# A graph network kernel: the work ahead of the first one-hots put in one tied order

## The chip, the cores and the metric

The kernel runs on one core of a Trainium2 chip. The core has a matrix engine (TensorE, "PE" in the profile, its weight loads listed apart as "PEld"), a vector engine (VectorE, "DVE"), a scalar engine (ScalarE, "ACT"), GpSimd ("POOL", used here for index patterns and for indirect DMAs) and SyncE ("SP", used here only to issue DMAs). Each engine takes its instructions in the order in which the program was laid out. Time is device microseconds (us) of one execution. Before the change the median of 7 runs is 885.18 us, the lowest 883.09, the highest 887.0.

## The reference

Two graph layers stand one behind the other, on 6250 nodes with 64 features and 206250 edges, which are sorted by destination. The first layer is two graph convolutions, the second a message network; both need sums over the edges of a node.

```python
h = jnp.maximum(_layernorm(x, axis=-1), 0.0)
x = x + _L0_gnn_ref(h, edge_index, ...)      # two convolutions
h = jnp.maximum(_layernorm(x, axis=-1), 0.0)
x = x + _L1_gnn_ref(h, edge_index, ...)      # messages, their sum, an update

def _gin_conv(x, src, dst, Wa, ba, Wb, bb):
    agg = jax.ops.segment_sum(x[src], dst, num_segments=N)
    h = x + agg
    h = jax.nn.relu(h @ Wa + ba)
    return h @ Wb + bb

message = node_features[source]
y = _mlp3(message, WM1, bM1, WM2, bM2, WM3, bM3)
z = jax.ops.segment_sum(y, destination, num_segments=node_features.shape[0])
```

Every sum over edges is a product with one matrix A, whose element (source, destination) is the number of edges between the two. A has 6250 by 6250 elements.

## The kernel before

The nodes are cut into 49 tiles of 128 (`NT`). For each tile t of destinations the kernel builds its 49 blocks of A in bytes (`build`, L433), adds the first convolution's sum from them (`FirstSum`, L576) and stores the blocks to DRAM. Two later sweeps load A again for the other two sums (L760); they take the time from about 366 us on and are not touched.

**How a tile of A is built.** The edges of 64 pairs of nodes (`G`) are turned into one-hots on VectorE by `hot` (L404): "there" (L411), "high" (L415) and "low" (L418), one instruction each for a whole tile, and in three pieces of 16, 16 and 32 for tile 0 (`FIRST_HOTS`). TensorE multiplies low by high: 64 small matmuls for a tile in four groups of 16 (L443, "counts"). ScalarE copies each group out of PSUM (L445). After each group `between` issues one quarter of the previous tile's sum (L586, 12 or 13 matmuls with the values `hp`), and whatever stands in the table `beside` under that group's number, 4 t + i.

**Where the one-hots come from.** The edges of two tiles are found in these steps, for batches of 1, 2, 2, ... pairs of tiles (`BATCHES`): `search` (L301) compares every 550th destination with the tile's bounds on ScalarE and gets a row number on VectorE (L313, L314); `fetch_blocks` (L317) gathers that row by an indirect DMA on POOL; `search_block` (L326) compares again on ScalarE; `fetch_edges` (L337) works out the offset on VectorE and gathers 128 destinations and sources by indirect DMAs (`d_win`, `s_win`); `slots` (L353) turns them into numbers by 9 to 11 VectorE instructions; `cast` (L389) copies two of the three numbers to bf16 on ScalarE; `turn` (L394) transposes them on TensorE, and ScalarE copies the result to `lkw` (L402), which `hot` reads. Batch 0 feeds tiles 0 and 1, batch 1 tiles 2 to 5.

**Where `hp` comes from.** The 49 tiles of x are taken in seven chunks of 7 (`values`, L507). `norm` (L232) is the layernorm: mean, a scale, the difference, a square on ScalarE, its sum, a root on ScalarE, a reciprocal, and the last product, so six VectorE instructions with two trips to ScalarE. `split` (L250) then writes h as three bf16 parts into `hp`: three ScalarE copies and, between them, products of TensorE with the identity (L256, fp32) and with minus the identity (L258) that leave the remainder. A product holds one of the two "cnt" buffers in PSUM, which the counts use too. Quarter 0 of a sum needs chunks 0 and 1, quarter 3 needs chunks 5 and 6.

**What sets the order.** The program is written as a list of calls; a planner at compile time places each instruction on its engine when, by its own estimates, its inputs are ready, earlier calls first. `behind(op, other)` ties an instruction behind another on the same engine without any wait at run time. `follow` ties one behind the newest count, copy or one-hot that is recorded in `counted`. At the start of the program (L546 to L572) come searches, the layernorm chunks 0 to 4 and the slots of batch 0, with few ties; chunks 5 and 6 come after tile 0 has been built, and the slots of batch 1 are in `beside` under the first group of tile 0.

Of the kernel before, what the change touches and what calls it, by code (L numbers as in the profile page):

```python
# [146 lines left out]
def load_x(nc, xs, x, engines):  # L147
# [5 lines left out]
    engines[0].dma_start(xs[:N - full * P, full, :], x[full * P:])  # L153
# [3 lines left out]
def fast(ctx: ExitStack, tc: tile.TileContext, x, src, dst, w, bad, out):  # L157
# [16 lines left out]


# [6 lines left out]
    load_x(nc, xs, x, [nc.sync, nc.scalar])  # L182
# [12 lines left out]
    nc.vector.tensor_scalar(ident_a, w.ident, 1.0 / UNIT, None, op0=OP.mult)  # L195
# [12 lines left out]
    nc.vector.tensor_copy(smp_f, smp_i)  # L208
# [23 lines left out]
    def norm(to, t, n):  # L232
# [10 lines left out]
        nc.vector.tensor_reduce(var, sq, axis=AX.X, op=OP.add)  # L243
        nc.scalar.activation(var, var, AF.Sqrt, bias=w.eps, scale=1.0 / D)
        nc.vector.reciprocal(var, var)
        nc.vector.scalar_tensor_tensor(to, xm, 0.0, var[:, :, None].to_broadcast([P, n, D]), op0=OP.max, op1=OP.mult)  # L246
        return begun, centered, squared

    def split(parts, h):
# [4 lines left out]
        for i in range(2):  # L254
            ps = banks[:, i].rearrange("p (t d) -> p t d", d=D)
            nc.tensor.matmul(ps, w.ident, h, start=True, stop=False)  # L256
# [26 lines left out]
    counted, swept = {}, []  # L283

    def behind(op, other):

        tc.add_manual_dep(op.ins, other.ins.name,
                          mybir.DependencyInfo(mybir.DependencyClass.NoSync, mybir.DependencyReason.DATA),
                          reason="order on an engine")
        return op  # L290
# [46 lines left out]
    def fetch_edges(b):  # L337
# [4 lines left out]
        nc.vector.scalar_tensor_tensor(off_f[:, qs], sign2[:, qs], -0.5, base[:, qs], op0=OP.mult, op1=OP.add)  # L342
# [10 lines left out]
    def slots(b):  # L353
# [12 lines left out]
        def first(op):  # L366
            follow(op, "DVE")

# [17 lines left out]
        nc.vector.tensor_tensor(byte, byte, shift, op=OP.logical_shift_left)  # L386
# [7 lines left out]
    def turn(b, i):  # L394
# [4 lines left out]
        for k in range(3):  # L399
            follow(nc.tensor.transpose(ps[:, k * P:(k + 1) * P], parts2[b % 2][:, i, k, :], identb), "PE")  # L400
# [3 lines left out]
    def hot(lkw, g0, n):  # L404

        def of(i):
# [4 lines left out]
        nc.vector.tensor_tensor(there, word2[:, None, :, :].to_broadcast(shape),  # L411
                                of(0)[:, :, None, :].to_broadcast(shape), op=OP.is_equal)
# [7 lines left out]
            of(2)[:, :, :, None].to_broadcast([P, n // 2, 2, W]), op=OP.mult)  # L420
        return low.bitcast(F8), high
# [10 lines left out]
    def build(t, between):  # L432
# [3 lines left out]
        for g0, m in FIRST_HOTS if t == 0 else ((0, G),):  # L436
            low, high = hot(lkw, (t % 2) * G + g0, m)
# [68 lines left out]

    def values(t):  # L507
        h = work.tile([P, XT, D], FP, name="h")
        begun, centered, squared = norm(h, t, XT)
        if t <= XT:  # L510
            behind(begun, sampled)
            behind(begun, bounds)
# [530 lines left out]
```

## Time and profile before

| | |
|---|---|
| median of 7 runs | 885.18 us (883.09 to 887.0) |
| the profiled execution | 884.99 us, of which the span of the trace is 882.3 us |
| busy, share of the span | TensorE 853.2 us, 97%; its weight loads 731.9 us, 83%; VectorE 629.9 us, 71%; ScalarE 570.4 us, 65%; POOL 122.5 us, 14% |
| lines that cost TensorE most | L760 (sweeps), L586 (first sums, 237.1 us), L443 (counts, 113.6 us), L256 (products of h, 17.5 us) |
| first group of counts starts | 33.37 us |
| tile 0's last copy of counts | 39.69 us |

The span begins with the first instruction and ends with the last; 2.7 us of the execution lie outside it. "Low of tile t" below is the last of the three one-hot instructions of a tile; its end is when the tile's counts can start. Averages over the whole span say little about the first 60 us, so the lines that matter are those of stretches of a few microseconds.

### The profile page before, as it was taken

How to read it: one execution, taken by the hardware profiler on the slowest of the kernel's cores; microseconds unless marked ns; L12 is line 12 of the kernel's file. 1: busy time of each engine (PE TensorE's matmuls, PEld its weight loads, DVE VectorE, ACT ScalarE, POOL GpSimd, SP SyncE). 2: the span in 40 equal slices, each digit the busy share in tenths (PEclk: the TensorE clock that was granted, in tenths of full speed). 3: DMA queues.
4: the chain of work that ended last, by engine and by line, in shares of the span. 5: the costliest groups of instructions: out<-in, count | busy, mean ns of one | idle time of the engine just before them, and what ended most of it. 6: DMA issues, size and time to landing. Idle time of an engine off the chain costs nothing.

```text
span 882.3 us, 19764 instructions
## 1 busy us (share of the span) xinstructions
PE 853.2 (97%) x8251; PEld 731.9 (83%) x8251; DVE 629.9 (71%) x933; ACT 570.4 (65%) x775; POOL 122.5 (14%) x86
## 2 busy tenths in 40 slices
PE   3799999999999999999999999999999999999997
PEld 1489999999999999888888878888889877777785
DVE  6999999999999998635554545554556686767672
ACT  5776777776776666655555555546546578878773
POOL 4537732324421200000000000000000000000000
PEclk9899999999999999999999999999999999999998
DMA  6336555455544543734444444334434567877772
GB/s 147 111 113 183 149 162 150 138 149 172 161 138 126 144 126 112 232 97 136 120 123 132 122 123 122 124 111 133 132 89 130 176 217 230 247 231 229 246 209 60
DMA packets 148326, 133.57 MB, mean 151 GB/s; under 512 B 29988, under 2 KB 110500, under 8 KB 148228
## 3 DMA queue, kind: packets, MB, share of 16 engines
q1 hardware_dynamic: 141784, 121.19, 46.3%
q0 software_dynamic: 3600, 10.32, 4.0%
q8 instruction: 66, 1.08, 0.5%
q10 hardware_dynamic: 2844, 0.72, 0.4%
q14 instruction: 32, 0.26, 0.1%
HBM read 91.25 MB, written 40.94 MB: 150 GB/s over the span
## 4 chain that ended last, share of the span: by engine, by line
PE 82%; DVE 6%; DMA 5%; ACT 4%; issue 1%; SPq 0%; POOL 0%; ACTq 0%; DVEq 0%; POOLq 0%
PE acc L760 42%; PE acc L586 20%; PE cnt L443 8%; PE ps_t L465 5%; DMA a<-A 4%; PE ps_y L474 3%; ACT ar L753 3%; DVE low L418 1%; PE ps_g L504 1%; DVE high L415 1%; DMA blk<-in_dst_dram,row 1%; DVE there L411 1%; PE cnt L256 1%; DVE ar L753 1%; DMA xs<-in_x_dram 1%
## 5 line engine op out<-in xcount | busy, mean ns | idle before, releaser
L753 DVE CAST ar<-a 128x2048 fp32r<-128x2048 uint8 (+1 forms) x200 | 220.1, 1110 | 183.5 <-PE acc L760 158.5
L753 ACT CAST ar<-a 128x2048 fp32r<-128x2048 uint8 (+2 forms) x126 | 232.4, 1846 | 123.8 <-PE acc L760 107.5
L760 PE MATMUL acc<-ar,h2r 128*128 128x512 f32 (+2 forms) x1274 | 297.6, 388 | 0.0
L760 PEld LDWEIGHTS acc<-ar,h2r 128*128 128x128 f32 x1274 | 229.3, 188 | 49.8 <-issue 5.8
L586 PE MATMUL acc<-hp,a 128*128 128x193 bf16 x2401 | 237.1, 248 | 0.4 <-ACT a L445 0.2
L445 ACT ACTIVATE a<-cnt 128x784 int16<-128x784 f32 x196 | 161.0, 822 | 70.0 <-PE cnt L443 69.8
L586 PEld LDWEIGHTS <-a 128*128 128x128 fp8e4 x2401 | 196.8, 98 | 2.6 <-issue 0.8
L760 PE MATMUL acc<-ar,yr 128*128 128x512 f32 (+2 forms) x637 | 157.6, 399 | 0.0
L760 PEld LDWEIGHTS acc<-ar,yr 128*128 128x128 f32 x637 | 115.7, 189 | 32.5 <-issue 10.1
L443 PEld LDWEIGHTS <-low 128*128 128x128 fp8e4 x3136 | 107.0, 96 | 9.4 <-issue 8.2
L443 PE MATMUL cnt<-high,low 128*128 128x49 bf16 x3136 | 113.6, 186 | 1.0 <-DVE low L418 0.5
L418 DVE TENSOR_TENSOR low<-there,lkw 128x2048 int32<-128x2048 bf16 (+2 forms) x51 | 112.1, 2197 | 0.0
L415 DVE TENSOR_TENSOR high<-high,lkw 128x3136 bf16<-128x3136 bf16 (+2 forms) x51 | 87.8, 1721 | 16.0 <-PE cnt L443 15.5
L322 POOL DMA_INDIRECT blk<-in_dst_dram,row x25 | 58.8, 2353 | 99.8 <-DVE base L314 87.3
L411 DVE TENSOR_TENSOR there<-word,lkw 128x2048 bf16<-128x2048 bf16 (+2 forms) x51 | 58.9, 1173 | 0.0
L347 POOL DMA_INDIRECT s_win<-in_src_dram,off x25 | 35.3, 1413 | 7.6 <-issue 7.6
L347 POOL DMA_INDIRECT d_win<-in_dst_dram,off x25 | 26.1, 1043 | 65.1 <-DVE pair L370 48.5
L256 PE MATMUL cnt<-h,ident 128*128 128x448 f32 x28 | 17.5, 725 | 11.5 <-DVE h L246 10.1
L467 ACT ACTIVATE t<-ps_t,d 128x512 f32<-128x512 f32 (+2 forms) x26 | 17.3, 664 | 11.2 <-PE ps_t L465 11.1
L467 ACT ACTIVATE t<-ps_t,c 128x512 f32<-128x512 f32 (+1 forms) x26 | 17.2, 663 | 9.1 <-PE ps_t L465 9.1
L333 ACT ACTIVATE junk<-blk,below_node 128x550 bf16<-128x550 int32 x25 | 18.7, 748 | 3.4 <-DMA blk<-in_dst_dram,row 3.4
L256 PEld LDWEIGHTS cnt<-h,ident 128*128 128x128 f32 x28 | 5.4, 232 | 17.9 <-issue 5.7
(125 smaller groups left out, 611.9 us busy)
## 6 DMA issues: line engine op xcount, KB each, us to landing
a<-A SPq DMA_DIRECT2D x276, 256.0 KB, 2.8
A<-a SPq DMA_DIRECT2D x49, 768.0 KB, 4.2
a<-A SPq DMA_DIRECT2D x24, 192.0 KB, 2.6
a<-A SPq DMA_DIRECT2D x22, 64.0 KB, 2.4
out_dram<-o SPq DMA_DIRECT2D x11, 128.0 KB, 3.0
A<-a SPq DMA_DIRECT2D x49, 16.0 KB, 3.9
xs<-in_x_dram ACTq DMA_DIRECT2D x3, 224.0 KB, 6.0
xs<-in_x_dram SPq DMA_DIRECT2D x3, 224.0 KB, 6.3
```

The lines of the kernel that those rows point to most:

```text
L322: nc.gpsimd.indirect_dma_start(out=blks[q], out_offset=None, in_=dst.rearrange("(r b) -> r b", b=BLK), in_offset=bass.IndirectOffsetOnAxis ...
L347: nc.gpsimd.indirect_dma_start(out=win[:, i, :], out_offset=None, in_=of.rearrange("(a o) -> a o", o=1), in_offset=bass.IndirectOffsetOnAx ...
L411: nc.vector.tensor_tensor(there, word2[:, None, :, :].to_broadcast(shape), of(0)[:, :, None, :].to_broadcast(shape), op=OP.is_equal)
L415: nc.vector.tensor_tensor(high, high2[:, None, :, :].to_broadcast(shape), of(1)[:, :, None, :].to_broadcast(shape), op=OP.is_equal)
L418: counted["DVE"] = nc.vector.tensor_tensor(low.rearrange("p (g i) w -> p g i w", i=2), there.rearrange("p g w i -> p g i w"), of(2)[:, :, ...
L443: counted["PE"] = nc.tensor.matmul(ps[:, b, j * H:(j + 1) * H], low[:, g, :], high[:, g // 2, :, g % 2], start=True, stop=True)
L445: counted["ACT"] = nc.scalar.activation(a[:, :, k:k + 2 * PG].rearrange("p h (b j) -> p h b j", b=2), ps[:, :, :PG * H].rearrange("p b (j ...
L465: placed(nc.tensor.matmul(ps[:, :n * P], wt, rhs, start=(i == 0), stop=(i == len(terms) - 1)))
L467: nc.scalar.activation(to, ps[:, :n * P], AF.Relu, bias=bias)
L586: nc.tensor.matmul(acc[:, t % 2, :], self.a[:, k, :], hp[:, k], start=(k == 0), stop=False)
L753: widen(ar.rearrange(f"p k t b -> {order}"), a.rearrange(f"p t (k b) -> {order}", b=P))
L760: op = nc.tensor.matmul(acc[:, :n * P], part, ar[:, k - k0].rearrange("p t b -> p (t b)"), start=(k == 0 and i == 0), stop=(k == H - 1 and ...
```

## The change

The change touches only the first two tiles' worth of work and leaves every computation as it was. It does these things:

- x is loaded on the two queues in the other order: chunks 0, 2, 4, 6 are issued by ScalarE, chunks 1, 3, 5 and the tail by SyncE.
- The first use of the sample of destinations (L208) is tied behind four small constants on VectorE.
- The products of h on TensorE (L256) are tied behind the newest transpose of `turn` and the newest count that has been issued by then.
- Chunks 0, 1 and 2 stay at the start, with chunk 0's mean behind the sample, its square behind the first search, and chunk 1's mean behind the first row number. Of chunk 3 only the mean and the difference stand ahead of the offsets of batch 1 and the slots of batch 0; its products come after batch 0's transposes.
- Chunk 4 is issued under the first group of tile 0: its mean behind the last slot instruction of batch 0, its variance behind the first low. The second piece of tile 0's one-hots is tied behind chunk 4's h.
- Chunk 5 is issued under the last group of tile 0, with its mean behind tile 0's last low. Chunk 6 is issued under the first group of tile 1, with its mean behind tile 1's low.
- The slots of batch 1, which stood under the first group of tile 0, are tied behind chunk 6's h; the casts and transposes of batch 1 move from tile 0's groups to groups 1 to 3 of tile 1.
- The searches and block searches of batches 2 and 3 move with them, into `beside` of tile 0.

The diff, cut to its core:

```diff
-    engines[0].dma_start(xs[:N - full * P, full, :], x[full * P:])
+    engines[-1].dma_start(xs[:N - full * P, full, :], x[full * P:])
...
-    load_x(nc, xs, x, [nc.sync, nc.scalar])
+    load_x(nc, xs, x, [nc.scalar, nc.sync])
...
-    nc.vector.tensor_scalar(ident_a, w.ident, 1.0 / UNIT, None, op0=OP.mult)
+    constants = nc.vector.tensor_scalar(ident_a, w.ident, 1.0 / UNIT, None, op0=OP.mult)
...
-    nc.vector.tensor_copy(smp_f, smp_i)
+    behind(behind(nc.vector.tensor_copy(smp_f, smp_i), constants), bounds)
...
-            nc.tensor.matmul(ps, w.ident, h, start=True, stop=False)
+            op = nc.tensor.matmul(ps, w.ident, h, start=True, stop=False)
+            for other in ("turn", "PE"):
+                if other in counted:
+                    behind(op, counted[other])
...
-    def fetch_edges(b):
+    def fetch_edges(b, before=None):
...
+        if before:
+            behind(op, before)
...
-    def slots(b):
+    def slots(b, before=None):
...
         def first(op):
             follow(op, "DVE")
+            if before:
+                behind(op, before)
...
+        counted["turn"] = op
...
-    def hot(lkw, g0, n):
+    def hot(lkw, g0, n, before=None):
...
+        if before:
+            behind(op, before)
...
-            low, high = hot(lkw, (t % 2) * G + g0, m)
+            low, high = hot(lkw, (t % 2) * G + g0, m, {0: normed[3][1], 16: normed.get(4, [None])[-1]}.get(g0) if t == 0 else None)
...
-    def values(t):
-        h = work.tile([P, XT, D], FP, name="h")
-        begun, centered, squared = norm(h, t, XT)
-        if t <= XT:
-            behind(begun, sampled)
-            behind(begun, bounds)
-            behind(squared, searched[0])
-        if t == XT:
-            behind(centered, searched[1])
-        split(hp[:, t:t + XT], h)
+    normed, hs = {}, {}
+
+    def values(c, *others, whole=True):
+
+        h = hs[c] = work.tile([P, XT, D], FP, name="h")
+        normed[c] = norm(h, c * XT, XT)
+        for op, other in zip(normed[c], others):
+            if other:
+                behind(op, other)
+        if whole:
+            parts_of(c)
+
+    def parts_of(c):
+        split(hp[:, c * XT:(c + 1) * XT], hs.pop(c))
...
-        at(0, slots, b + 1)
-        at(4, cast, b + 1, 0)
-        at(5, cast, b + 1, 2)
+        if b > 0:
+            at(0, slots, b + 1)
+        at(4 if b else 10, cast, b + 1, 0)
+        at(5 if b else 10, cast, b + 1, 2)
         for i in range(BATCHES[b + 1] if b + 1 < len(BATCHES) else 0):
-            at(7 + 2 * i, turn, b + 1, i)
+            at(7 + 2 * i if b else 12 + 2 * i, turn, b + 1, i)
...
-    values(0)
+    values(0, sampled, None, searched[0])
+    values(1, searched[1])
     search_block(0, 0)
     fetch_edges(0)
-    values(XT)
-    slots(0)
+    values(2)
+    for i in range(2):
+        op = search_block(1, i)
+    values(3, normed[2][-1], whole=False)
+    fetch_edges(1, normed[3][1])
+    slots(0, normed[3][1])
     cast(0, 0)
     cast(0, 2)
-    for i in range(2):
-        op = search_block(1, i)
-    fetch_edges(1)
     turn(0, 0)
-    values(2 * XT)
     search(2, op)
     fetch_blocks(2)
-    values(3 * XT)
-    search(3)
-    fetch_blocks(3)
-    values(4 * XT)
-    for i in range(2):
-        search_block(2, i)
-    fetch_edges(2)
+    parts_of(3)
+
+    def fourth():
+        normed[4] = None
+        values(4, counted["slots"], None, None, firsts[0])
+
+    def fifth():
+        values(5, counted["DVE"])
+
+    def sixth():
+        values(6, counted["DVE"])
+        slots(1, normed[6][-1])
+
+    beside[0] = [(fourth, ()), (search, (3,)), (fetch_blocks, (3,))] + beside.get(0, [])
+    beside[3] = [(search_block, (2, 0)), (search_block, (2, 1)), (fetch_edges, (2,)), (fifth, ())] + beside.get(3, [])
+    beside[4] = [(sixth, ())] + beside.get(4, [])
...
             if t == 0:
-                values(5 * XT)
                 for i in range(2):
                     search_block(3, i)
                 fetch_edges(3)
-                values(6 * XT)
                 search(4)
                 fetch_blocks(4)
```

More of the change, by code (lines that the diff above doesn't have):

```diff
@@ L173, in bank, with behind @@
         return pmix.tile([P, CH * 4 // mybir.dt.size(dtype)], dtype, tag="mix", name=name)
+    def behind(op, other):
+        tc.add_manual_dep(op.ins, other.ins.name,
+                          mybir.DependencyInfo(mybir.DependencyClass.NoSync, mybir.DependencyReason.DATA),
+                          reason="order on an engine")
+        return op
     root = const.tile([P, 1], FP, name="root")
@@ L242, in norm @@
         var = work.tile([P, n], FP, name="var", tag=f"var{n}")
-        nc.vector.tensor_reduce(var, sq, axis=AX.X, op=OP.add)
+        summed = nc.vector.tensor_reduce(var, sq, axis=AX.X, op=OP.add)
         nc.scalar.activation(var, var, AF.Sqrt, bias=w.eps, scale=1.0 / D)
         nc.vector.reciprocal(var, var)
-        nc.vector.scalar_tensor_tensor(to, xm, 0.0, var[:, :, None].to_broadcast([P, n, D]), op0=OP.max, op1=OP.mult)
-        return begun, centered, squared
+        ended = nc.vector.scalar_tensor_tensor(to, xm, 0.0, var[:, :, None].to_broadcast([P, n, D]), op0=OP.max, op1=OP.mult)
+        return begun, centered, squared, summed, ended
     def split(parts, h):
@@ L281, in tiles_of @@
         return range(starts[b], starts[b] + BATCHES[b]), slice(starts[b], starts[b] + BATCHES[b])
[L283 to L290, printed above, removed]
+    counted, firsts, swept = {}, [], []
     def follow(op, engine):
@@ L341, in fetch_edges @@
         each, qs = tiles_of(b)
-        nc.vector.scalar_tensor_tensor(off_f[:, qs], sign2[:, qs], -0.5, base[:, qs], op0=OP.mult, op1=OP.add)
+        op = nc.vector.scalar_tensor_tensor(off_f[:, qs], sign2[:, qs], -0.5, base[:, qs], op0=OP.mult, op1=OP.add)
+        if before:
+            behind(op, before)
         nc.vector.tensor_scalar(off[:, qs], off_f[:, qs], float(E - P), None, op0=OP.min)
@@ L385, in slots @@
         nc.vector.tensor_scalar(byte, byte, float(BYTE[1] - BYTE[0]), float(BYTE[0]), op0=OP.mult, op1=OP.add)
-        nc.vector.tensor_tensor(byte, byte, shift, op=OP.logical_shift_left)
+        counted["slots"] = nc.vector.tensor_tensor(byte, byte, shift, op=OP.logical_shift_left)
         numbers[b] = {0: word, 2: byte}
@@ L399, in turn @@
         for k in range(3):
-            follow(nc.tensor.transpose(ps[:, k * P:(k + 1) * P], parts2[b % 2][:, i, k, :], identb), "PE")
+            op = nc.tensor.transpose(ps[:, k * P:(k + 1) * P], parts2[b % 2][:, i, k, :], identb)
+            follow(op, "PE")
+        counted["turn"] = op
         lkw = lkws[starts[b] + i] = wins.tile([P, 3, P], BF, name="lkw", bufs=5)
         nc.scalar.copy(lkw.rearrange("p a b -> p (a b)"), ps[:, :3 * P])
-    def hot(lkw, g0, n):
+    def hot(lkw, g0, n, before=None):
         def of(i):
@@ L410, in hot @@
         there = hots.tile([P, G // 2, W, 2], BF, name="there")[:, :n // 2]
-        nc.vector.tensor_tensor(there, word2[:, None, :, :].to_broadcast(shape),
-                                of(0)[:, :, None, :].to_broadcast(shape), op=OP.is_equal)
+        op = nc.vector.tensor_tensor(there, word2[:, None, :, :].to_broadcast(shape),
+                                     of(0)[:, :, None, :].to_broadcast(shape), op=OP.is_equal)
+        if before:
+            behind(op, before)
         shape = [P, n // 2, H, 2]
@@ L420, in hot @@
             of(2)[:, :, :, None].to_broadcast([P, n // 2, 2, W]), op=OP.mult)
+        firsts.append(counted["DVE"])
         return low.bitcast(F8), high
```

## The prediction

> **What bounds the kernel now.** First the chain that ended last, in order of time. From 365 us on it is TensorE in the sweeps, which the change leaves alone; around 85 to 110 us it is TensorE's counts and first sums; between 57 and 85 us it is VectorE without a break:
>
> ```profile
> 59.61 0.34 DVE byte L386
> 59.95 1.13 DVE there L411
> 61.08 0.53 DVE r L594 x2
> 61.62 1.70 DVE high L415
> 63.32 2.20 DVE low L418
> ...
> 82.61 0.20 DVE byte L385
> 82.81 2.21 DVE low L418
> 85.02 0.05 issue
> 85.07 0.59 PE cnt L443 x16
> 85.66 1.11 PE acc L586 x13
> ```
>
> The reader sees that the low of tile 7, at 85 us, is what TensorE waits for last; after it TensorE never waits for a one-hot for long. So the end is set by when VectorE gets there. Second, VectorE's busy time in stretches (start:end, length, busy, instructions, clock, DMA share, GB/s):
>
> ```profile
> 5.40:12.00 6.60, 5.91 (x24) 1.00 0.87 152
> 12.00:26.00 14.00, 11.08 (x37) 1.00 0.45 122
> 26.00:33.00 7.00, 6.02 (x23) 1.00 0.51 155
> 33.00:40.00 7.00, 6.29 (x11) 0.76 0.18 56
> 40.00:45.00 5.00, 4.88 (x6) 0.66 0.58 161
> 45.00:51.65 6.65, 6.02 (x10) 1.00 0.10 30
> 51.65:60.00 8.35, 8.11 (x19) 1.00 0.60 175
> 60.00:84.93 24.93, 24.93 (x33) 1.00 0.55 161
> ```
>
> From the end of tile 2's low (49.37 + 2.28 = 51.65) to that of tile 7 VectorE idles 0.24 us in 33.3. Before it, from the landing of the sample at 5.4, it works 40.2 us and idles 6.05. Third, the timeline names those idle times and the waits of TensorE:
>
> ```profile
> 20.04 0.23 DVE L370 TENSOR_SCALAR pair<-d_win 128x128 int32<-128x128 int32 x1 [1.87 <-DMA d_win<-in_dst_dram,off]
> 32.06 1.02 PE L256 MATMUL cnt<-h,ident 128*128 128x448 f32 x2 [2.02 <-DVE h L246]
> 38.51 0.20 DVE L245 RECIPROCAL var<-var 128x7 f32<-128x7 f32 x1 [0.71 <-ACT var L244]
> 39.38 0.41 ACT L392 CAST parts<-byte 128x256 bf16<-128x256 int32 x1
> 40.40 0.48 ACT L402 COPY lkw<-ps_win 128x384 bf16<-128x384 bf16 x1
> 41.96 2.28 DVE L418 TENSOR_TENSOR low<-there,lkw 128x2048 int32<-128x2048 bf16 x1
> ```
>
> VectorE's 6.05 us are 0.53 for x, 0.69 for the first block, 1.87 for the destinations, 0.72, 0.71 and 0.63 for layernorm roots, and small ones. The counts of tile 0 are ready when the first low ends at 27.37, but start at 33.37, behind a product of h that waits 2.02 us. TensorE idles 2.89 + 1.31 + 0.41 + 0.26 = 4.9 us between 26 and 53.5.
>
> **The sum is made at one place:** low of tile 2 ends at 51.65 now. What follows to 84.93 is the same VectorE work in both kernels, so a later or earlier low of tile 2 moves the end by as much, as long as TensorE keeps up.
>
> **The parts in front.** Four constants leave the path between the sample and its product: 5.63 to 6.12, a gain of 0.5. The first search wins 0.2 more, since its row (L313, 9.85) waits now behind a mean. Chunk 0 of x is issued on ScalarE's queue at 0.74 instead of SyncE's at 1.81, landing 6.0 us after issue, so near 6.7 instead of 7.17. ScalarE issues one load more (0.44 to 0.84 each, ending about 3.4); it is idle until 8.38, so this costs nothing. SyncE's later weight loads come about 1.1 us sooner, and would cost only if they slowed the first gather (landing 3.9). The two gathers then cost what they did (10.28 to 14.15; 15.74 to 20.02), and the first slot instruction starts near 19.1 instead of 20.04. Slots of batch 0 run 1.9 us without the h, sum and difference that stand between them now (0.61 + 0.60 + 0.61), so they end near 21.2 instead of 23.64; cast, transposes and copy take 1.6 to 2.2 (23.64 to 25.87). The first low ends near 25, its counts start near 25.2 instead of 33.37, and tile 0 is counted some 6 us earlier. That is what the change does; it frees TensorE, not VectorE.
>
> **The part that costs.** The slots of batch 1 run now between 27.3 and 33.5, their copy is there at 40.88, and tile 2's one-hots wait for nothing. Afterwards they are behind chunk 6's h, and that chunk's mean is behind tile 1's low. So from tile 1's low to tile 2's this stands in a row:
> - chunk 6: mean to scale 0.66, scale to difference 0.20 (9.11, 9.77, 9.97), difference 0.61, square 0.57, sum 0.61, root 0.28, reciprocal 0.20, h 0.62, and five hand-overs of about 0.04: 3.95;
> - slots for two tiles: 77.80 to 79.29 and 0.20 + 0.21 + 0.20 + 0.41: 2.5;
> - cast, transposes, copy: 39.38 to 40.88, and 0.32 from copy to "there" (25.55 to 25.87), 0.05 in front: 1.87;
> - one-hots 1.14 + 1.70 + 2.28: 5.1.
>
> The sum is 13.4 us, against 51.65 - 44.24 = 7.41 now. VectorE is idle in it for square and root (1.0) and the 1.87, with little else that may run: chunk 5's last steps, offsets and rows. To break even tile 1's low has to end at 38.2 instead of 44.24.
>
> **The balance.** Idle time of VectorE up to tile 2's low, taken (and bounds):
> 1. for x: 0.5 (0.3 to 0.6), row 0.53.
> 2. up to the first slot: 2.9 (2.0 to 3.8), rows 0.69 and 1.87. The wait is 0.9 us shorter, but chunk 1's mean may not start before the first row number, so less stands ready.
> 3. for the first copy of `lkw`: 0.3 (0 to 0.8); chunk 4's mean and difference and chunk 3's end (about 2.6) cover the 2.2.
> 4. chunk 4's and 5's roots: 0.5 (0.2 to 1.5). They cost 2.45 with small ones now; the one-hots that are not tied fill them.
> 5. chunk 6: 1.3 (0.5 to 2.3): the 1.0, and one copy of counts (0.83) that may stand ahead of its square on ScalarE, less what fills it.
> 6. the turn of batch 1: 2.9 (1.6 to 4.5): the 1.87, and what TensorE has in front of the transposes. Chunk 6's product becomes ready with the same h (from 47.74 to 51.1 now: 3.4 us), the slots and cast take 2.9 of that; a quarter (1.02) may stand there as well.
>
> Together 8.4 (4.6 to 13.5) instead of 6.05. Work: 40.2 - 0.5 for the constants, + 1.0 because steps that depend on each other start after the full duration (0.61) and not after 0.53 as interleaved ones do (10.50 to 11.03); some 13 such steps: 40.7 (39.7 to 41.0). Tile 2's low ends at 5.4 + 40.7 + 8.4 = 54.5, or 2.9 us later. Against the profiled execution (884.99; span 882.3 and 2.7 around it) that is 887.9. That execution lies 0.2 under the median of the runs, so the forecast is 885.18 + 2.9 = 888.1. The likeliest case alone spans 887 to 890.5.
>
> **TensorE's cover.** The products move with the chunks and cost nothing, because TensorE will be ahead: tile 1's quarters (4.3 us), which stand after tile 2's first counts now, come before them. If that cover went (half clock, or counts and two products sharing the two "cnt" buffers), the cost would be what exceeds 4.3. A pair of product passes takes 1.02 at 32.06 and 1.86 at 34.16, while the clock row shows 0.76 and 0.66. Were chunks 3 to 6 all at the slow rate, TensorE would do 4 x 2 x 0.84 = 6.7 us more than at the fast one; part of it is paid now.
>
> [...]
>
> **Rivals.**
> - Faster: the gain on the first counts goes through. It decides where tile 2's low ends before 49.9 (1.8 us earlier), which needs an idle total of at most 3.8, or 4.8 with the work at its lower bound; the lower bounds sum to 4.6. So: the turn at 1.6 and chunk 6's waits filled by chunk 5's last steps, and a first wait under 2. For it: 2.45 us of root waits vanish. Against it: the 1.87 us after the slots have no cover. TensorE's 4.9 us of idle time are its ceiling, 880.3; I would expect 882.
> - No change: an idle total near 5.5, as the waits named in front go and those of chunk 6 and batch 1 come: 5.4 + 40.7 + 5.5 = 51.6, so 885.2. For it: tile 1's low at 38 to 38.5 is possible, since its work is 7 us nearer the front.
> - Much slower: the transposes of batch 1 stand behind tile 1's third group of counts, which needs a "cnt" buffer while chunks 5 and 6 hold them 3 to 4 us each, and behind two products and two quarters. Item 6 goes to 4.5 and 5 to 2.3, item 2 to 3.6: idle total 11.7, low at 57.8, 891.3.
>
> **How the numbers follow.** Chances: forecast 0.46, much slower 0.20, no change 0.20, faster 0.14. A difference of 0.2% (1.8 us) is about what a measurement of this kernel tells from none. So slower 0.66, same 0.20, faster 0.14. The range 883.5 to 892 leaves out about 0.1 at either end: most of the faster case, and the upper part of the much slower one.
>
> **What would show it.** Right: first counts near 25 us, tile 0's last copy near 33; tile 1's low near 39 to 41; then the two root waits of chunk 6 on VectorE, and a gap of 2 to 4 us ahead of tile 2's "there", released by ScalarE's `lkw`; tile 2's low near 54.5 and VectorE on the chain up to about 88. Wrong: tile 2's low before 50, or VectorE no longer on the chain after it, so that TensorE alone sets the end; or the first slot later than 20, because the gathers land later.

## The result, and the profile after

The changed kernel takes 891.12 us (median of 17 runs, 888.5 to 893.94), the kernel before beside it 885.0 (42 runs, 882.58 to 888.38): a ratio of 1.007, 95% interval 1.0061 to 1.008. In a second group of runs, with the experiments, it took 890.58 (6 runs) beside 886.32 (24 runs): 1.0048, interval 1.003 to 1.0067. So it is slower by 0.5 to 0.7%, 4.3 to 6.1 us, where 2.9 were forecast. Its first profiled execution took 887.86 us with a span of 885.8, which is below every one of the 17 runs; the profiled execution of the second group took 890.61, span 888.5. Both are read here, since they differ in the place that matters.

All engines of the first execution of the changed kernel by stage; the columns are start:end, length, then busy time (and instructions) of TensorE, its weight loads, VectorE, ScalarE and POOL, then TensorE's clock, DMA share and GB/s. The cuts are the landing of the sample, the first copy of `lkw`, the lows of tiles 1, 2 and 7, and chunk 6's reciprocal:

```profile
4.47:12.00 7.53, 1.85 (x3) 0.76 (x4) 5.81 (x19) 3.71 (x10) 2.28 (x3) 1.00 1.01 204
12.00:25.60 13.60, 11.82 (x26) 4.31 (x27) 9.09 (x33) 10.50 (x28) 7.52 (x8) 1.00 0.50 137
25.60:38.79 13.19, 9.85 (x112) 6.35 (x110) 13.09 (x22) 11.81 (x28) 3.38 (x4) 1.00 0.34 98
38.79:45.13 6.34, 3.95 (x22) 2.15 (x23) 3.40 (x13) 3.52 (x8) 4.24 (x4) 0.73 0.25 70
45.13:56.74 11.61, 10.49 (x129) 8.12 (x126) 9.12 (x20) 6.07 (x13) 6.08 (x6) 1.00 0.51 147
56.74:88.11 31.37, 27.35 (x530) 26.36 (x530) 31.37 (x48) 20.68 (x36) 15.34 (x6) 1.00 0.45 129
```

VectorE is nearly full while it builds tiles 0 and 1 (13.09 of 13.19), half idle in the 6.3 us after tile 1's low, and has another 2.5 us of idle time before tile 2's low, which ends at 56.74 instead of 51.65. From the landing of the sample to that low it works 40.51 us and idles 11.76 (52.27 - 40.51), where it worked 40.20 and idled 6.05 before. The timeline names the idle time (the number in brackets is the wait ahead of the instruction, and what ended it):

```profile
8.29 0.15 DVE L316 TENSOR_SCALAR row<-sign 128x1 int32<-128x1 f32 x1 [1.56 <-ACT junk L312]
13.21 0.16 DVE L345 SCALAR_TENSOR_TENSOR off_f<-sign,base 128x1 f32<-128x1 f32 x1 [0.52 <-ACT junk L336]
16.16 0.20 DVE L252 RECIPROCAL var<-var 128x7 f32<-128x7 f32 x1 [0.91 <-ACT var L251]
18.17 0.63 DVE L253 SCALAR_TENSOR_TENSOR h<-xm,var 128x448 f32<-128x448 f32 x1 [1.81 <-PE cnt L263]
20.19 0.22 DVE L377 TENSOR_SCALAR pair<-d_win 128x128 int32<-128x128 int32 x1
25.55 0.42 DVE L420 TENSOR_TENSOR there<-word,lkw 128x512 bf16<-128x512 bf16 x1 [0.33 <-ACT lkw L411]
28.27 0.58 PE L455 MATMUL cnt<-high,low 128*128 128x49 bf16 x16
42.21 0.62 DVE L250 TENSOR_REDUCE var<-sq 128x7 f32<-128x448 f32 x1 [0.64 <-ACT sq L248]
45.13 0.20 DVE L252 RECIPROCAL var<-var 128x7 f32<-128x7 f32 x1 [2.30 <-ACT var L251]
51.20 1.23 DVE L420 TENSOR_TENSOR there<-word,lkw 128x2048 bf16<-128x2048 bf16 x1 [2.28 <-ACT lkw L411]
54.45 2.29 DVE L429 TENSOR_TENSOR low<-there,lkw 128x2048 int32<-128x2048 bf16 x1
```

The first counts start at 28.27 instead of 33.37, and tile 1's low ends at 38.79 instead of 44.24, so the first two tiles do come sooner. The loads and the sample in front are not what does it: 0.95 us of the gain is a sample that landed at 4.47 instead of 5.42, and from the sample to the first slot the changed kernel takes 15.72 us (16.40 in the second execution) where the kernel before took 14.62. Then come chunk 6's waits (0.64 and 2.30) and the wait for batch 1's `lkw` (2.28), and tile 2 is 5.1 us late.

**Where the gain of the front went.** TensorE's busy time shows it. The rows are start:end, length, busy (instructions), clock, DMA share, GB/s; first of the kernel before, then of the changed one:

```profile
0.00:28.00 28.00, 13.19 (x29) 1.00 0.56 125
28.00:57.00 29.00, 24.12 (x270) 0.88 0.38 110
57.00:72.00 15.00, 15.00 (x291) 1.00 0.53 154
72.00:92.00 20.00, 19.53 (x367) 1.00 0.56 164
```

```profile
0.00:28.00 28.00, 15.16 (x32) 1.00 0.62 144
28.00:57.00 29.00, 23.01 (x266) 0.94 0.40 116
57.00:72.00 15.00, 11.03 (x230) 1.00 0.28 82
72.00:92.00 20.00, 20.00 (x374) 1.00 0.65 184
```

TensorE has worked 2.0 us more by 28 us. It is ahead, runs dry when tile 2 is late, and idles 4.0 us between 57 and 72, where it had not idled at all. By 92 us it is 71.84 - 69.20 = 2.6 us behind, and the first product of the sweeps starts 3.3 us later (the kernel before, then the changed one):

```profile
371.32 1.17 PE L760 MATMUL acc<-ar,h2r 128*128 128x512 f32 x4
```

```profile
374.63 1.17 PE L786 MATMUL acc<-ar,h2r 128*128 128x512 f32 x4
```

From 365.77 to 370 us the kernel before still adds up its last tile, so the sweeps begin somewhat later than the 365 and 366 us given ahead of the result. Of the 6.1 us between the medians of the first group the first trace shows these 3.3; the second trace, whose sweeps start at 376.29, shows 5.0, where the medians of its group differ by 4.3. The chain of waits (start, duration, what) says the same: it leaves VectorE after tile 3's low, where it stayed on VectorE up to 85 us before, goes through ScalarE's copies of the counts, and is TensorE's alone from 69.69:

```profile
62.52 2.21 DVE low L429
...
64.78 0.60 PE cnt L455 x16
...
65.40 0.82 ACT a L457
...
68.92 0.72 ACT a L457
...
69.69 0.43 PE acc L614 x3
```

**What the rest of the program adds.** From the first product of the sweeps to the end of the span the profiled executions of both kernels and all variants take 511.0 to 516.4 us, with no relation to the change. That spread is larger than most differences looked for here, so the variants below are judged by their medians first, and by the start of the sweeps in their one profile second. The sample of destinations lands between 4.36 and 6.81 us, by chance too.

### The profile page after: what moved, and what is told of

It is laid out like the page before. It is cut to its first block, busy times and chain, and to the rows that moved or that the text cites. A ratio compares the mean times of both kernels' runs of the same rounds, so it can differ in the third digit from the quotient of the medians.

```text
span 885.8 us, 19761 instructions
## 1 busy us (share of the span) xinstructions
PE 853.1 (96%) x8251; PEld 731.1 (83%) x8251; DVE 631.2 (71%) x933; ACT 570.8 (64%) x775; POOL 117.9 (13%) x86
## 4 chain that ended last, share of the span: by engine, by line
PE 90%; DVE 4%; ACT 3%; DMA 2%; issue 1%; ACTq 0%; SPq 0%; DVEq 0%
PE acc L786 45%; PE acc L614 21%; PE cnt L455 9%; PE ps_t L477 6%; PE ps_y L486 4%; DMA a<-A 1%; PE cnt L263 1%; PE ps_g L516 1%; DVE low L429 1%; ACT ar L779 1%; DVE high L426 1%; PE tf L468 1%; ACT a L457 1%; DVE ar L779 0%; DMA smp_i<-in_dst_dram 0%
## 5 line engine op out<-in xcount | busy, mean ns | idle before, releaser
L352 POOL DMA_INDIRECT s_win<-in_src_dram,off x25 | 33.3, 1331 | 8.1 <-issue 7.3
L479 ACT ACTIVATE t<-ps_t,e 128x512 f32<-128x512 f32 (+2 forms) x28 | 17.5, 630 | 2.9 <-PE ps_t L477 2.9
```

The costliest lines, as they stand in the source:

```text
L352: nc.gpsimd.indirect_dma_start(out=win[:, i, :], out_offset=None, in_=of.rearrange("(a o) -> a o", o=1), in_offset=bass.IndirectOffsetOnAx ...
L479: nc.scalar.activation(to, ps[:, :n * P], AF.Relu, bias=bias)
```

## The experiments

Theory 1: the row of steps between tile 1's low and tile 2's (chunk 6, slots, cast, transposes, copy, one-hots), none of which has cover, costs the time. Rivals: the ties of TensorE's products; TensorE's idle time alone; the clock. The profiled executions, in us from the start of the span, with the median of all runs. There are four groups of runs, the later three on chips 5, 6 and 1, the first without a chip on record; the kernel before has medians of 885.0, 886.27, 886.0 and 886.32 in them, and each ratio is taken within one group. The ratio is not always the quotient of the two medians: for the busy kernel on chip 6 it is 1.0055, where the medians give 1.0034:

| kernel | sample | low of tile 1 | low of tile 2 | first product of the sweeps | median | ratio to the kernel before (95%) |
|---|---|---|---|---|---|---|
| before | 5.42 | 44.24 | 51.65 | 371.32 | 885.0 | |
| changed, first group | 4.47 | 38.79 | 56.74 | 374.63 | 891.12 | 1.0061 to 1.008 |
| changed, chip 1 | 4.67 | 39.23 | 58.44 | 376.29 | 890.58 | 1.003 to 1.0067 |
| late slots alone | 6.18 | 42.38 | 58.09 | 377.11 | 891.34 | 1.0045 to 1.0092 |
| ties of the products alone | 4.50 | 43.91 | 51.33 | 370.99 | 886.54 | 0.9987 to 1.0019 |
| front alone | 5.91 | 42.84 | 50.25 | 369.91 | 883.83 | 0.9972 to 1.0008 |
| slots back | 5.27 | 43.00 | 50.76 | 377.61 | 893.64 | 1.0074 to 1.0115 |
| three buffers for h | 6.81 | 39.86 | 59.06 | 379.34 | 888.98 | 1.001 to 1.0044 |
| both early | 5.01 | 42.26 | 49.87 | 372.29 | 885.75 | 0.9986 to 1.0017 |
| transposes first | 6.21 | 40.66 | 57.61 | 375.64 | 888.54 | 1.0023 to 1.0052 |
| busy, chip 6 | 4.82 | 39.08 | 55.88 | 373.73 | 889.02 | 1.0035 to 1.0075 |
| busy, chip 1 | 4.79 | 39.42 | 56.29 | 375.26 | 890.4 | 1.0031 to 1.0069 |
| front, three buffers, ties | 4.96 | 44.19 | 51.84 | 371.51 | 886.22 | 0.998 to 1.0009 |
| front, three buffers | 4.36 | 44.54 | 52.01 | 371.66 | 886.06 | 0.9983 to 1.0013 |

**One part of the change alone: late slots.** The kernel before with chunk 6 behind tile 1's low, batch 1's slots behind its h, and their casts and transposes in tile 1's groups:

```diff
-                values(6 * XT)
...
+    def sixth():
+        values(6 * XT)
+        slots(1, hdone[6])
+
+    beside[4] = [(sixth, ())] + beside.get(4, [])
```

> The kernel before with one part of the change alone: chunk 6's mean behind tile 1's low, the slots of batch 1 behind chunk 6's h, its casts and transposes under tile 1's groups. Theory 1: tile 1's low comes somewhat earlier than 44.24, since the slots leave its front (41.5 to 43), but tile 2's low follows it 13.4 us later at least (17.95 in the changed kernel), so at 56 to 60, and the end is 5 to 8 us later than before: 890 to 893. Theory 2: the end stays near 885.

Measured 891.34 us, ratio 1.0069 (1.0045 to 1.0092): the whole loss of the change, from this one move. Tile 1's low to tile 2's takes 15.7 us instead of 7.4, and VectorE's wait stands where the changed kernel has it:

```profile
52.55 1.23 DVE L414 TENSOR_TENSOR there<-word,lkw 128x2048 bf16<-128x2048 bf16 x1 [2.15 <-ACT lkw L405]
```

Theory 1 holds for where the loss comes from. The clock is not needed for it: the products of chunks 5 and 6 all take 0.99 to 1.02 us a pair here, and the counts from 43.16 to 51.47 take 0.57 to 0.58 us a group, where the group at 35.46, behind the slow pair of chunk 4 (1.86), took 0.87.

**Another part alone: the products behind the counts.** The kernel before with chunk 4's products behind the first counts, and every product tied behind the newest count:

```diff
-            nc.tensor.matmul(ps, w.ident, h, start=True, stop=False)
+            follow(nc.tensor.matmul(ps, w.ident, h, start=True, stop=False), "PE")
...
-    values(4 * XT)
+    h4 = values(4 * XT, False)
...
+    beside[0] = [(split, (hp[:, 4 * XT:5 * XT], h4))] + beside.get(0, [])
```

> The kernel before with one part of the change alone: chunk 4's products stand behind the first group of counts, and every product behind the newest count. The first counts start at 28 to 29 us instead of 33.37. Theory 1 (VectorE sets the end, TensorE's idle time in front costs nothing): VectorE's lows of tiles 2 to 7 stay within 1 us and the end within 1 us of 885. Rival (TensorE's 4.9 us of idle time in front are what the end waits for): the end comes 3 to 5 us earlier, 880 to 882.

Measured 886.54, ratio 1.0003 (0.9987 to 1.0019): no change. The first counts start at 28.26, five microseconds earlier than before, and nothing comes of it. Tile 2's low is where it was (51.33). Counting tile 0 sooner only moves TensorE's idle time to a later place, and the rival by which TensorE's idle time in front is the bound falls.

**The front alone.** The kernel before with x on the queues in the changed order and the sample's use behind the four constants:

```diff
-    engines[0].dma_start(xs[:N - full * P, full, :], x[full * P:])
+    engines[-1].dma_start(xs[:N - full * P, full, :], x[full * P:])
...
-    load_x(nc, xs, x, [nc.sync, nc.scalar])
+    load_x(nc, xs, x, [nc.scalar, nc.sync])
...
-    nc.vector.tensor_copy(smp_f, smp_i)
+    behind(behind(nc.vector.tensor_copy(smp_f, smp_i), constants), bounds)
```

> The kernel before with one part of the change alone: x on the two queues in the other order, and the first use of the sample behind the constants. The prediction counted 0.5 us for the constants and 0.5 for x, and VectorE sets the end: 884 to 885 against 885 of the kernel before, a gain of 0.5 to 1.0. If the shorter front only makes VectorE wait elsewhere, no change.

Measured 883.83, ratio 0.999 (0.9972 to 1.0008): in the direction expected, and inside the noise. Two kernels built on it, which follow at the end, did not confirm it.

**Undo the late slots.** The changed kernel with batch 1's slots, casts and transposes back under tile 0's groups:

```diff
-        values(6, counted["DVE"])
-        slots(1, normed[6][-1])
+        values(6, counted["DVE"])
...
-        if b > 0:
-            at(0, slots, b + 1)
-        at(4 if b else 10, cast, b + 1, 0)
-        at(5 if b else 10, cast, b + 1, 2)
+        at(0, slots, b + 1)
+        at(4, cast, b + 1, 0)
+        at(5, cast, b + 1, 2)
```

> The changed kernel with one part undone: the slots, casts and transposes of batch 1 stand again under tile 0's groups, as before the change. Theory 1 (the row chunk 6, slots of batch 1, transposes, one-hots of tile 2 stands alone on VectorE and sets the end): tile 1's low comes 2.5 us later than the 38.79 of the changed kernel, for the slots that move ahead of it, and tile 2's low follows it by about 8 to 9 us instead of 17.95, so at 49 to 51 against 56.74; the end is 6 to 8 us earlier than the changed kernel's 891.1, so 883 to 885. Theory 2 (the ties of the products, or what the change does before the first one-hots, costs the time): at most 1 us of the 6 comes back, so 890 to 891.

A miss: 893.64, ratio 1.0094 (1.0074 to 1.0115), slower than the changed kernel. Tile 2's low came as expected, at 50.76, but the end went the other way. The timeline of this kernel shows why:

```profile
53.06 0.29 DVE L384 TENSOR_SCALAR high_i<-s_win 128x256 int32<-128x256 int32 x1 [1.38 <-DMA s_win<-in_src_dram,off]
53.87 0.62 DVE L253 SCALAR_TENSOR_TENSOR h<-xm,var 128x448 f32<-128x448 f32 x1
54.63 0.99 PE L263 MATMUL cnt<-h,ident 128*128 128x448 f32 x2 [3.70 <-DVE h L253]
56.57 1.86 PE L263 MATMUL cnt<-h,ident 128*128 128x448 f32 x2
59.76 0.57 PE L455 MATMUL cnt<-high,low 128*128 128x49 bf16 x16 [0.21 <-ACT hp L269]
60.37 1.79 DVE L426 TENSOR_TENSOR high<-high,lkw 128x3136 bf16<-128x3136 bf16 x1 [2.14 <-PE cnt L455]
```

The planner now spread chunk 6's steps over the one-hots of tile 2 (mean at 43.59, sum at 50.67) and put its h among batch 2's slots, and these wait for a gather that had moved back with the searches (batch 2's first gather of edges starts at 43.95). Chunk 6's h is ready at 54.5; its products stand in front of the rest of tile 1's counts, which hold the one-hot buffers that VectorE needs at 60.37. TensorE works 18.46 us between 28 and 57 where it worked 24.12 before. So an early low of tile 2 is not enough: chunk 6 has to come early as well. This kernel does not tell how much of that is chunk 6's place behind tile 1's low and how much the planner's spreading of its steps.

**Both early.** To test that reading: batch 1's slots right behind tile 0's last low, and chunk 6 next to chunk 5, ahead of tile 1's one-hots, with a third buffer for h:

```diff
     def fifth():
         values(5, counted["DVE"])
+        values(6, normed[5][1])
...
+    beside[3] = [(slots, (1,)), (cast, (1, 0)), (cast, (1, 2)), (turn, (1, 0)), (turn, (1, 1)),
...
+        h = hs[c] = work.tile([P, XT, D], FP, name="h", bufs=3)
```

> The changed kernel with the slots, casts and transposes of batch 1 right behind tile 0's last low, chunk 6 right behind chunk 5's mean and difference, both ahead of tile 1's one-hots, and three buffers for h. The front, the ties of the products and chunk 4's place stay as changed. If the late place of both (slots of batch 1 and chunk 6) is the whole loss, tile 1's low comes at 45 to 46, tile 2's at 50 to 51.5 as before the change, no wait for a copy of lkw ahead of tile 2, TensorE does not wait 3 us for chunk 6's h as it did with the slots alone put back (3.70), and the end is at 884 to 886. If the front's own waits (5.1 us of VectorE up to the first slot against 3.1 before) count as well, 887 to 888.

Measured 885.75, ratio 1.0002 (0.9986 to 1.0017): as expected, the loss is gone. The front, the ties of the products and chunk 4's place are still in this kernel, so they do not bring the loss by themselves. Its clock is 0.82 in the mean from 28 to 57 us (0.88 in the kernel before, 0.94 in the changed one), and the pairs at 43.53, 46.37 and 48.77 take 1.83, 1.86 and 1.70; that costs it nothing that the median shows. The third buffer may have a part in the result; the next experiment has it alone. Tile 2's low ends at 49.87, 1.8 us earlier than before. No gain follows: a new wait stands behind it, for the halves of a weight that ScalarE makes late, and tile 3's low ends at 61.02 instead of 59.62:

```profile
56.09 0.29 DVE L274 TENSOR_TENSOR w1p<-w1x,w1p 128x128 fp32r<-128x128 f32 x1 [2.07 <-ACT w1p L273]
```

**A third buffer for h.** In the changed kernel chunk 2's h waits 1.81 us at 18.17 for a product of TensorE, since h has two buffers.

```diff
-        h = hs[c] = work.tile([P, XT, D], FP, name="h")
+        h = hs[c] = work.tile([P, XT, D], FP, name="h", bufs=3)
```

> The changed kernel with three buffers for h instead of two, nothing else. In the trace of the changed kernel the h of a chunk waits 1.81 us at 18.17 for TensorE's product that still reads the buffer, and the first slots stand behind it. If that wait is what eats the earlier chain, the first slot starts near 18.5 instead of 20.19, the first low ends 1 to 1.8 us earlier, and as all later work on VectorE hangs on it, tile 2's low and the end too: about 889.5. If the wait is only one of several that give way to each other, the first slot starts within 0.5 us of now and the time stays at 891.

Measured 888.98, ratio 1.0027 (1.001 to 1.0044), which is 2 to 4 us under the changed kernel by the ratios (1.0048 and 1.007; other groups of runs). That wait is gone from the trace, and the first slot starts 14.62 us after the sample instead of 15.72 and 16.40. Its profiled execution was the slowest of its twelve (894.8), with the sample landing at 6.81 and a wait for `lkw` of 4.89, so it does not show how the gain reaches the end.

**The transposes of batch 1 ahead of chunk 6's products.** In the changed kernel the transposes stand on TensorE behind both, and ScalarE's copy of `lkw` behind the copies of these products:

```diff
     def sixth():
-        values(6, counted["DVE"])
+        values(6, counted["DVE"], whole=False)
         slots(1, normed[6][-1])
+        parts_of(5)
...
+    beside[6] = beside.get(6, []) + [(parts_of, (6,))]
```

> The changed kernel with the products of chunks 5 and 6 written later in the program: chunk 5's after chunk 6's layernorm, chunk 6's after batch 1's first transposes. The row on VectorE stays; what goes is what stood in it by queues: chunk 6's root behind chunk 5's copies on ScalarE (VectorE waited 2.30 us for it), and batch 1's transposes behind chunk 6's products on TensorE (VectorE waited 2.28 us in one trace, 4.89 in that with three buffers). If these queues are what makes the row 17.95 us instead of the 13.4 of the prediction, tile 2's low follows tile 1's by 14 to 15 us, and the end is 3 to 4 us earlier than the changed kernel's 891.1: 887 to 888. If the row costs by its own length alone, 891.

Measured 888.54, ratio 1.0037 (1.0023 to 1.0052), somewhat above the expected 887 to 888, and by the ratios 1 to 3 us under the changed kernel, again in other groups of runs. The wait for `lkw` is 1.27 instead of 2.28; chunk 6's root still waits 2.30.

**The clock.** The two profiled executions of the changed kernel show the same idle time of TensorE before chunk 5's product, and then different clocks. TensorE's rows (start:end, length, busy, clock, DMA share, GB/s), first of the first execution, then of the second:

```profile
40.00:42.50 2.50, 1.32 (x2) 0.68 0.09 27
42.50:45.00 2.50, 2.50 (x21) 0.64 0.19 52
45.00:47.50 2.50, 1.87 (x15) 1.00 0.35 112
47.50:50.00 2.50, 2.46 (x40) 1.00 0.54 164
```

```profile
40.00:42.50 2.50, 0.89 (x3) 1.00 0.22 56
42.50:45.00 2.50, 2.28 (x20) 0.64 0.19 46
45.00:47.50 2.50, 1.87 (x5) 0.50 0.24 54
47.50:50.00 2.50, 2.50 (x22) 0.50 0.65 219
```

In steps of 0.4 us the clock is at 0.50 from 40.9 to 44.3 in the first, and from 43.2 to 50.0 in the second. The timelines of the two, of TensorE, ScalarE and VectorE:

```profile
41.18 1.83 PE L263 MATMUL cnt<-h,ident 128*128 128x448 f32 x2 [3.23 <-DVE h L253]
43.42 0.54 ACT L269 CAST hp<-cnt 128x448 bf16<-128x448 f32 x1 [1.24 <-PE cnt L268]
44.09 0.83 ACT L457 ACTIVATE a<-cnt 128x784 int16<-128x784 f32 x1
44.80 0.29 ACT L251 ACTIVATE var<-var,eps 128x7 f32<-128x7 f32 x1
50.68 0.49 ACT L411 COPY lkw<-ps_win 128x384 bf16<-128x384 bf16 x1
```

```profile
41.61 0.99 PE L263 MATMUL cnt<-h,ident 128*128 128x448 f32 x2 [3.22 <-DVE h L253]
43.43 1.86 PE L263 MATMUL cnt<-h,ident 128*128 128x448 f32 x2 [0.22 <-ACT hp L269]
46.78 1.82 PE L263 MATMUL cnt<-h,ident 128*128 128x448 f32 x2
52.40 0.48 ACT L411 COPY lkw<-ps_win 128x384 bf16<-128x384 bf16 x1
52.91 1.23 DVE L420 TENSOR_TENSOR there<-word,lkw 128x2048 bf16<-128x2048 bf16 x1 [4.88 <-ACT lkw L411]
```

In the first the slow pair comes early and makes ScalarE late for chunk 6's root (44.80), which stands in its queue behind the copy of chunk 5's product; VectorE's wait there is 2.30. In the second the slow pairs come later, the root waits 1.05, and the copy of `lkw` is late instead: VectorE waits 4.88 for it. The next kernel fills TensorE's wait, with 12 products that nothing uses (an addition to the computation; its results are left alone):

```diff
+    def busy():
+        ps = bank("ps_busy")
+        for i in range(12):
+            behind(nc.tensor.matmul(ps[:, :448].rearrange("p (t d) -> p t d", d=D), minus, hp[:, 0:7, :D],
+                                    start=True, stop=True), counted["quarter"])
+
+    beside[5] = [(busy, ())] + beside.get(5, [])
```

> The changed kernel with 12 matmuls that nothing uses (448 columns of bf16, 0.19 us each, 2.3 us in all) in the 3.22 us in which TensorE waits for chunk 5's h at 38 to 41 us. They make no work shorter. If the slow passes after that wait (1.83 us for a pair at 41.18 against 1.02 elsewhere, counts 0.87 against 0.58) come from the wait itself, the products of chunks 5 and 6 run in 1.02, chunk 6's root and batch 1's transposes come 1 to 3 us sooner, and the end is 1 to 3 us earlier than 891.1, with a smaller spread of the runs. If the slow passes have nothing to do with the wait, 891, or a little later for the added work.

Measured 889.02, ratio 1.0055 (1.0035 to 1.0075); all pairs of chunks 5 and 6 run at 0.99 to 1.02 us, and the root waits 1.04. That looked like 2 us, but the changed kernel's 891.12 was of another group of runs. So both were run on one chip, the changed kernel and the busy one:

> The changed kernel itself, unaltered, beside the next kernel on one chip. 890 to 892 us, or 0.5 to 0.7% above the kernel before, on any theory; it is there so that the next kernel is compared with it directly.

> The changed kernel with 12 products that nothing uses, in TensorE's wait for chunk 5's h. Theory 1 (the slow passes after that wait are a part of the loss): 1 to 3 us below the changed kernel of the same chip. Rival (the clock is nothing for the time, and the first look at this kernel differed by the chip): within 0.8 us of it.

Measured 890.58 (6 runs) and 890.4 (7 runs). The rival's value: no gain in the time. In the busy kernel's profile the pairs of chunks 5 and 6 were fast again:

```profile
41.82 0.99 PE L263 MATMUL cnt<-h,ident 128*128 128x448 f32 x2 [0.87 <-DVE h L253]
43.63 1.02 PE L263 MATMUL cnt<-h,ident 128*128 128x448 f32 x2 [0.21 <-ACT hp L269]
```

Its tile 2 is 2.15 us and its sweeps 1.0 us earlier than those of the changed kernel beside it, but its sweeps then took 514.8 us against 512.2. What is shown: in both executions of the changed kernel 3.2 us of idle time are followed by a half clock, and in both of the busy kernel, where TensorE idles at most 0.92 us at a time there, none follows (all pairs take 0.99 to 1.02, and the clock of the second is 1.00 from 28 to 57 us); between the two executions of the changed kernel VectorE's wait for `lkw` differs by 2.6 us (4.88 against 2.28). With all pairs of chunks 5 and 6 at 0.99 to 1.02 the way from tile 1's low to tile 2's still takes 16.80 and 16.87 us in the busy kernel, and 15.71 with the late slots alone, against 17.95 and 19.21 in the changed kernel and 7.41 before, so the clock is the smaller part of it. What is not shown is that filling the wait makes the kernel faster. The intervals of the two ratios would leave room for some 2 us either way, so this stays open.

**A version that beats both?** The free parts put together on the kernel before: the front, and three buffers for h, with the ties of the products and without them.

```diff
-        h = work.tile([P, XT, D], FP, name="h")
+        h = work.tile([P, XT, D], FP, name="h", bufs=3)
```

> The kernel before with what was free in the change: the queues of x and the sample's use behind the constants, products of h behind the newest count with chunk 4's behind the first counts, and three buffers for h. Batch 1's slots and all chunks of the layernorm stay where the kernel before has them. Theory 1 (the end follows the low of tile 2, and the front is worth 0.5 to 1 us, the third buffer up to 1.0 more): 883 to 885 us. Rival (what the front gains is given back later): 885 to 887.

> The kernel before with the queues of x, the sample's use behind the constants, and three buffers for h, without the ties of the products. Theory 1: the 1.0 us that VectorE waited for a buffer of h at 25 us with the front alone is gone, 883 to 884.5 us. Rival (that wait is filled again by the next one): 884.5 to 886.

Measured 886.22, ratio 0.9995 (0.998 to 1.0009), and 886.06, ratio 0.9998 (0.9983 to 1.0013). Both are misses for theory 1 and the rivals' outcome: no change. In the second the wait for a buffer of h is gone, but the first mean waits 1.74 us for x at 7.50, the first slot 1.58 for its destinations at 19.42, and tile 2's low ends at 52.01. In this execution the early sample (4.36) is given back at the next transfers. No version was found that beats the kernel before.

## Why the prediction was right, and where not

**The sign and the mechanism: right, the size too small.** The forecast was 888.1 us, 2.9 slower, because the slots and chunk 6 stand in a row behind tile 1's low; measured 891.12, 6.1 slower (4.3 in the second group), and the late slots alone give the whole loss. The time lies inside the range, but outside the 887 to 890.5 given for the likeliest case alone, and near the "much slower" rival (891.3). The term that was too small is the balance of idle time. That the time still fell inside the range is partly luck: tile 2's low came 5.1 and 6.8 us late instead of 2.9, and not all of that was handed on to the end.

**The work: right, with two errors that cancel.** 40.7 us was taken for VectorE up to tile 2's low, 40.51 and 40.30 were measured in the two executions. Of these 0.4 are two halves of a weight (L274, at 52.34), which stood behind tile 2's low before and which the sum did not have; the 1.0 us that it added for steps that depend on each other was too much.

**The balance of idle time: too low.** 8.4 was taken (4.6 to 13.5), 11.76 and 13.47 were measured. The rival's total was 11.7. By items, with the second execution behind the first:
- Item 1, for x: taken 0.5, and nothing over 0.1 in the first execution: chunk 0's mean starts at 5.25, where x was expected at 6.7.
- Item 2, up to the first slot: taken 2.9 (2.0 to 3.8), measured 1.56 + 0.52 + 0.31 + 0.91 + 1.81 = 5.1, then 5.8. This is the largest error, and outside the bound. The sum had the row number and the destinations in it, but not that the chunks run into h's two buffers. The changed order brings chunks 0 to 2 so close that chunk 2's h waits for a product (1.81, 1.52), and the ties leave nothing else to run. The third buffer removed this wait. So the first slot is at 20.19, and 21.07 in the second, not 19.1. A first slot later than 20 had been named as a sign of being wrong, with gathers that land later as the reason; here it waits for no gather.
- Item 3, the first `lkw`: taken 0.3, measured 0.33 in the first and nothing in the second; chunk 3's h waits another 0.42 and 0.43 ahead of it.
- Item 4, chunks 4 and 5: taken 0.5. The timeline has no root wait of theirs; the small idle times that remain in the first execution, 0.7 us in all, are not in the items.
- Item 5, chunk 6: taken 1.3 (0.5 to 2.3), measured 0.64 + 2.30 = 2.9, then 0.64 + 1.05 = 1.7. The bound had one copy of counts ahead of the square; in the first execution a copy of chunk 5's product and one of counts stand ahead of the root, and the former waits 1.24 for a product that took 0.58 at a clock of 0.50 (42.80; 0.36 at 47.10, at 1.00).
- Item 6, the turn of batch 1: taken 2.9 (1.6 to 4.5), measured 2.28, then 4.88. Right within its bounds in one, above them in the other, where the pairs at 43.43 and 46.78 took 1.86 and 1.82.

**The row of 13.4 us from tile 1's low to tile 2's:** measured 17.95 and 19.21. The 4.5 us on top in the first execution are 1.97 from the end of chunk 6's sum to its root, 0.87 for offsets, rows and chunk 5's sum ahead of chunk 6's mean, 0.45 for chunk 5's last steps between chunk 6's scale and its difference, 0.41 more for the turn, 0.41 for the two halves of a weight, and 0.35 more for the slots. In the second execution it is 0.72 to the root and 3.0 more for the turn. Only the waits were in the balance (items 5 and 6); chunk 5's last steps, offsets and rows were counted on to fill idle time, and about 1.3 us of them stood in the row instead. The chain that ended last runs in the first execution from 41.18 to 52.28 through TensorE's products, counts and sums and ScalarE's copies, and not through the slots.

**Tile 1's low at 39 to 41:** 38.79, just ahead of that, and 39.23, with the sample 0.95 and 0.75 us early. Its gain of 5.45 us was more than the forecast, and yet short of the break-even.

**First counts near 25.2:** wrong, 28.27. The first slot was 1.1 us late. The slots ended at 22.91 instead of 21.2, because offsets and the sum of chunk 3 (20.96) still ran between them. A product pair at 23.16 stood ahead of the last transpose of batch 0, so the first low ended at 27.07. Another pair (27.03) and its products stood ahead of the counts, 1.2 us more.

**"A later low of tile 2 moves the end by as much":** wrong in size. Tile 2's low is 5.1 and 6.8 us late, the sweeps 3.3 and 5.0. TensorE had worked 1.1 to 2.0 us more by 28 us. VectorE is on the chain only up to tile 3's low at 64.7, and not to 88; from 69.69 on TensorE decides, and that VectorE leaves the chain the prediction had listed as a sign against itself. The two errors have opposite signs: more delay at tile 2, and less of it handed on. The undone slots showed the limit of this step from the other side: tile 2's low at 50.76 and the sweeps 6.3 us late.

**TensorE's cover of the products:** not as said. The products had their 4.3 us of cover for TensorE's own work, but they also stand ahead of batch 1's transposes and of ScalarE's copies in the queues, which VectorE waits for. This way a slow pair (1.82 to 1.86 us, where a fast one takes 0.99 to 1.02) reaches VectorE without TensorE being the bound: chunk 6's root waits 2.30 in the first execution and 1.05 in the second, and the wait for `lkw` is 2.28 and 4.88. The 890.5 at the upper end of the likeliest case lies 2.4 us above the forecast, as much as chunks 3 to 6 all at the slow rate (6.7) would exceed the cover (4.3); no run shows this term. What the runs showed in its place: the four pairs of chunks 3 and 4 took 1.02 us each in both executions, and the four pairs of chunks 5 and 6 took 4.98 us in the first and 5.74 in the second, where the busy kernel took 4.02. Filling the wait changed the median by 0.2 us, with room for some 2 us either way, so the slow pairs are seen in the trace, and a price of theirs is not shown in the time.

**The faster rival and the "no change" one** needed a turn of 1.6 us and chunk 6's waits filled. Neither was filled: in the 6.3 us behind tile 1's low VectorE had 3.40 us of work that was allowed to run.

## What to carry to other kernels

Moving work behind an instruction that the bound engine waits for is dear when the moved work makes trips to other engines: count every step of the row, the hand-overs, and what stands ahead in the other engines' queues, and ask what else may run there; here it was 3.40 us of work in the first 6.34. A stage that starts five microseconds earlier can be worth nothing, as the ties alone showed, if the engine that it feeds then runs dry, so look for the place where that engine waits next, and for the last place at which it waits at all. If a program's tail varies by more than the effect, compare the point in the trace where the changed part ends, and compare medians of one group of runs before a difference of two microseconds is believed.

## What the runs showed of the hardware

- The stretch at half clock began and ended at different places in two executions of the changed kernel. After the same idle time of 3.2 us the clock was at 0.50 from 40.9 to 44.3 us in one execution, and from 43.2 to 50.0 in another, where the first pair of passes was still fast (0.99 us) and the next ones took 1.86 and 1.82. So the stretches are 3.4 and 6.8 us long.
- The idle time ahead of a slow pair was 1.75 us in the kernel with the transposes first (then 1.83 us for a pair), and 1.64 with the late slots alone (1.86). The same length of 2.02 us is followed by a fast pair (1.02) in the kernel before, and by a slow one (1.86) in the front with three buffers. The slow pairs at 34.16 in the kernel before (1.86) and at 41.18 in the changed one (1.83) lie where the clock row shows 0.50; at the start of the program, where the row shows 1.00, a pair takes 1.83 as well (11.77 in the changed kernel), and no run here says why.
- The landing of a 1.5 KB load issued at the start of the program varied from 4.36 to 6.81 us, and the sweeps from 511.0 to 516.4 us, in executions of nearly the same program.
